# One Haar axis moved from TensorE to VectorE, whole 256-point transforms by channel, and plain products and sums for GpSimd in between

**Chip, cores, metric.** The kernel runs on one core of a Trainium2 chip, in fp32. The metric is the device time of one execution in microseconds (us); smaller is better. Every time is a median of several executions of one program. Runs have a state (fast or slow, by the clock that was granted).

## The reference

Four layers act on x[4, 64, 256, 256] one after the other. Layers 0, 2 and 3 are long convolutions of each image; layer 1 thresholds in the Haar domain.

```python
def _L0_conv_ref(x, ...):                      # layers 2 and 3 alike
    hx, hy = _implicit_filter(...), _implicit_filter(...)   # small sine networks
    k = einsum('ijk,imk->ijmk', hx, hy)[0]     # an outer product for every channel
    y = irfft2(rfft2(x, s=(512, 512)) * k_f)[..., :256, :256]
    return y + x * bias[:, None, None]

def _L1_conv_ref(x, v, conv_w, tau):
    f1 = haar2d(x)                             # 256-point Haar, both axes
    acc = 0
    for i in range(2):
        f3 = f1 * v[i]                         # v, tau: [256, 256]
        f4 = einsum('bchw,oc->bohw', f3, conv_w[i])        # 64 channels mixed
        acc = acc + sign(f4) * relu(abs(f4) - tau[i])
    return haar2d(acc, inverse=True) + x
```

One step of the Haar transform replaces a row by the sums and the differences of its even and odd elements, times 1/sqrt(2), and goes on with the sums: 128 pairs, 64, ... 1.

## The kernel before

As the filters are outer products, a convolution is two triangular matrix products, one per axis. Data are transposed by each product that has the image as the stationary operand. There are three phases with DRAM between them. **A**, by channel (four images): layer 0 (stages a1, a2) and two 128-point Haar products (a3, a4). **B**, by rows of coefficients, with (2 row groups x 64 channels) on the partitions: the "butterflies" that make a 256-point transform of two halves, then the products with v, the mixing of channels on TensorE, the thresholds, the sums. **C**, by channel: the inverse Haar products and layers 2 and 3.

```python
# Phase A: four stages on TensorE, eight PSUM buffers with one tag
hr = keep("ah")
for b, ps in enumerate(stage("a3")):
    haar_stationary(ps, x1[b], haarT)          # contracts rows, transposes
    nc.scalar.copy(hr[b], ps)
for b, ps in enumerate(stage("a4")):
    haar_moving(ps, hr[b], haarT)              # contracts rows, keeps the layout
    nc.vector.tensor_copy(fs[:, b], ps)
...
# Phase B, one step: 2 rows of either group, four units of 128 x 1024; PSUM bufs=4
butterfly(ft, r0, "fwd")
for b in range(B):
    f1 = ft[:, 2 * b : 2 * b + 2]...
    for i in range(2):
        nc.gpsimd.tensor_tensor(f3, f1, vts[:, i, :], ALU.mult)
        ... matmul f4 <- mix, f3
        nc.scalar.activation(m, f4, AF.Abs)
        nc.scalar.activation(f4, f4, AF.Sign)
        nc.vector.tensor_tensor(m, m, vts[:, 2 + i, :], ALU.subtract)      # two SBUF inputs
        nc.vector.scalar_tensor_tensor(m, m, 0.0, f4, ALU.max, ALU.mult)
    nc.vector.tensor_tensor(acc, ms[0], ms[1], ALU.add)
    nc.gpsimd.tensor_tensor(gt..., acc, f1, ALU.add)
butterfly(gt, r0, "inv")
```

Tiles are named by a tag, and a tag has `bufs` buffers that are used in turn. The order of the instructions of each engine, and the waits, are made when the program is built: an instruction of a later step can be placed ahead of one that stands earlier in the text.

Of the kernel before, what the change touches and what calls it, by code (L numbers as in the profile page):

```python
"""Four sequence-mixing layers on images x[b, c, 256, 256].

Layers 0, 2 and 3 convolve each image with a filter that is an outer product
hx x hy (zero padded to twice the length, so nothing wraps): out = Tx X Ty^T + bias X
with lower triangular Toeplitz matrices. Layer 1 works in the Haar domain: the
256-point transform is two 128-point transforms and a butterfly between their
scaling coefficients, and as it is orthogonal, "inverse(acc) + x" is
inverse(acc + forward(x)).

Phase A, by channel: layer 0 and the 128-point transforms of both axes.  # L10
Phase B, by rows of coefficients, channels on partitions: the butterflies, the
channel mixing, the soft thresholds, the inverse's butterflies.
Phase C, by channel: the 128-point inverse transforms, layers 2 and 3.
A product with the image as the stationary operand contracts its rows and leaves
it transposed, so two of them treat both axes.
"""
# [10 lines left out]
F32 = mybir.dt.float32  # L27
# [11 lines left out]
# A filter's period in DRAM, zeros after it, and how often it stands there.  # L39
PERIOD = N + P  # L40
REPEATS = 23
ROWS = 2
# [10 lines left out]
def conv_haar_kernel(ctx: ExitStack, tc: tile.TileContext, x, zT, w1, wbd, cols, decay, bias, haar, mixT, vt, out):  # L53
# [5 lines left out]
    haar_sb = const.tile([P, 2, P], F32, tag="haar", name="haar_sb")  # L59
    nc.sync.dma_start(haar_sb, haar)  # L60
    haarT = haar_sb[:, 0, :]
    haarN = haar_sb[:, 1, :]
# [9 lines left out]
    coef = dram.tile([B, C, N, N], F32, tag="coef", name="coef")  # L72
    mixed = dram.tile([B, C, N, N], F32, tag="mixed", name="mixed")
    filt = [dram.tile([P, REPEATS, PERIOD], F32, tag=f"filt{l}", name=f"filt{l}") for l in range(NL)]

    # The filters of all layers: x networks on partitions 0-63, y networks on 64-127.
    with tc.tile_pool(name="mlp", bufs=1) as mp, tc.tile_pool(name="mlp_ps", bufs=2, space=PSUM) as mps:
# [12 lines left out]
        for layer in range(3):  # L90
# [12 lines left out]
            # u less the nearest multiple of 2 pi, for the sine's range.  # L103
# [17 lines left out]
    def load_toeplitz(pool, l, c):  # L121
        """T[a, (x y), i] = h[i - a], with zeros for i < a: row a = 8 * a1 + a2 starts
        a1 periods less 8 and a2 periods less 1 behind the filter's first."""
        t = pool.tile([P, 2, N], F32, tag=f"toep{l}", name=f"toep{l}_{c}")
        for w in range(2):
            start = (w * C + c) * REPEATS * PERIOD
            src = bass.AP(filt[l].tensor, filt[l].offset + start, [[PERIOD - 8, 16], [PERIOD - 1, 8], [1, N]])
            nc.sync.dma_start(t[:, w, :], src)
        return t

    def toeplitz(ps, data, t, which):
        """ps[:, m, i] = sum over a of data[a, m] h[i - a]."""
        for m in range(2):
            cut = bass.ts(m, P)
            nc.tensor.matmul(ps[:, m, :], data[:, 0, cut], t[:, which, :], start=True, stop=False)  # L135
            nc.tensor.matmul(ps[:, m, HALF:], data[:, 1, cut], t[:, which, :HALF], start=False, stop=True)  # L136

    def haar_stationary(ps, data, mat):
        """Contracts data's rows and transposes it."""
        for m in range(2):  # L140
            for k in range(2):
                nc.tensor.matmul(
                    ps[:, m, bass.ts(k, P)], data[:, k, bass.ts(m, P)], mat, start=True, stop=True
                )

    def haar_moving(ps, data, mat):
        """Contracts data's rows and leaves its layout."""
        nc.tensor.matmul(ps, mat, data, start=True, stop=True)  # L148

    def images(ap, c):  # L150
        return [ap[b, c].rearrange("(k p) j -> p k j", p=P) for b in range(B)]

    # Phase A
    with (
        tc.tile_pool(name="a_in", bufs=3) as pin,
        tc.tile_pool(name="a_mid", bufs=6) as mid,
        tc.tile_pool(name="a_out", bufs=2) as pout,
        tc.tile_pool(name="a_ps", bufs=8, space=PSUM) as pps,
    ):
        for c in range(C):  # L160
            t0 = load_toeplitz(pin, 0, c)
            xs = pin.tile([P, B, 2, N], F32, tag="x", name=f"x_{c}")
            for b, src in enumerate(images(x, c)):
                nc.sync.dma_start(xs[:, b], src)
            fs = pout.tile([P, B, 2, N], F32, tag="f", name=f"f_{c}")

            def stage(name):
                return [pps.tile([P, 2, N], F32, tag="ps", name=f"{name}_ps{b}_{c}") for b in range(B)]

            def keep(name):  # L170
                return [mid.tile([P, 2, N], F32, tag=name, name=f"{name}{b}_{c}") for b in range(B)]

            cols_i = keep("ay")
            for b, ps in enumerate(stage("a1")):
                toeplitz(ps, xs[:, b], t0, 0)
                nc.scalar.copy(cols_i[b], ps)  # L176
            x1 = keep("ax")
            for b, ps in enumerate(stage("a2")):
                toeplitz(ps, cols_i[b], t0, 1)
                nc.vector.scalar_tensor_tensor(x1[b], xs[:, b], bias_sb[:, c : c + 1], ps, ALU.mult, ALU.add)  # L180
            hr = keep("ah")
            for b, ps in enumerate(stage("a3")):
                haar_stationary(ps, x1[b], haarT)
                nc.scalar.copy(hr[b], ps)
            for b, ps in enumerate(stage("a4")):
                haar_moving(ps, hr[b], haarT)
                nc.vector.tensor_copy(fs[:, b], ps)  # L187
            for b, dst in enumerate(images(coef, c)):
                nc.gpsimd.dma_start(dst, fs[:, b])  # L189

    # Phase B: a coefficient row is l = (h g r), h the transform's half; partitions are (g c).
    W = 2 * ROWS * N

    def rows_of(ap, g, r0):
        """[c, (b h), ROWS * N] of coefficient rows h * 128 + g * 64 + r0 ..."""
        start = g * (HALF // 2) + r0
        return [
            ap[b].rearrange("c (h l) k -> c h (l k)", h=2)[:, :, start * N : (start + ROWS) * N] for b in range(B)
        ]

    with (
        tc.tile_pool(name="b_in", bufs=2) as pin,
        tc.tile_pool(name="b_mid", bufs=2) as mid,
        tc.tile_pool(name="b_out", bufs=2) as pout,
        tc.tile_pool(name="b_ps", bufs=4, space=PSUM) as pps,
    ):

        def butterfly(t, r0, name):
            """Sums and differences of the halves' scaling coefficients, on both axes, in place."""
            pairs = t.rearrange("p n r (t q) -> p (n r) t q", t=2)[:, :, :, 0]  # L210
            sd = mid.tile([P, B * 2 * ROWS, 2], F32, tag="sd", name=f"{name}_{r0}")
            nc.vector.tensor_tensor(sd[:, :, 0], pairs[:, :, 0], pairs[:, :, 1], ALU.add)
            nc.vector.tensor_tensor(sd[:, :, 1], pairs[:, :, 0], pairs[:, :, 1], ALU.subtract)
            nc.vector.tensor_copy(pairs, sd)  # L214
            if r0 == 0:
                rows = t.rearrange("p (b h) r k -> p b h r k", h=2)[:C, :, :, 0, :]
                rsd = mid.tile([C, B, 2, N], F32, tag="rsd", name=f"{name}_r", bufs=1)
                nc.vector.tensor_tensor(rsd[:, :, 0, :], rows[:, :, 0, :], rows[:, :, 1, :], ALU.add)
                nc.vector.tensor_tensor(rsd[:, :, 1, :], rows[:, :, 0, :], rows[:, :, 1, :], ALU.subtract)
                nc.vector.tensor_copy(rows, rsd)  # L220

        for step in range(HALF // 2 // ROWS):
            r0 = step * ROWS
            ft = pin.tile([P, B * 2, ROWS, N], F32, tag="ft", name=f"ft_{step}")
            vts = pin.tile([P, 4, W], F32, tag="vt", name=f"vt_{step}")
            for g in range(2):
                part = slice(g * C, (g + 1) * C)
                nc.sync.dma_start(vts[part].rearrange("p q w -> p (q w)"), vt[step, g].partition_broadcast(C))
                for b, src in enumerate(rows_of(coef, g, r0)):
                    nc.sync.dma_start(ft[part, 2 * b : 2 * b + 2].rearrange("p h r k -> p h (r k)"), src)  # L230
# [163 lines left out]
```

## Time and profile before

| | before |
|---|---|
| median | 4529.9 us (4527.8 to 4534.3, four runs beside the changed kernel) |
| phase A, first to last TensorE stage | 1121.7 us, 17.5 per channel |
| phase B, first product to last sum | 1480.9 us, 11.57 per unit of 128x1024 (128 units) |
| phase C | 1792.4 us, 28.0 per channel |

The prediction below shows the slices, the windows and the timeline of one step. Names in all views: PE is TensorE, PEld its loading of stationary operands, DVE VectorE, ACT ScalarE, POOL GpSimd, SPq and ACTq the queues from which transfers (DMA) are issued. PSUM is the memory that the products write, SBUF the one that holds the other tiles. Here are two groups of instructions of B that it quotes only as numbers. Columns: line, engine, operation, output and inputs with shapes, count | busy us in total, mean ns of one | idle time of the engine before them and what ended it.

```profile
L238 POOL TENSOR_TENSOR f<-ft,vt 128x1024 f32<-128x1024 f32 x256 | 688.4, 2725 | 59.7 <-DVE ft L214 33.5 <-DMA vt<-in_vt 26.1
...
L245 DVE TENSOR_TENSOR m<-m,vt 128x1024 f32<-128x1024 f32 x256 | 585.2, 2296 | 317.6 <-ACT m L243 316.7
```

A product on GpSimd takes 2725 ns in the mean and VectorE's subtraction 2296 ns. Both means hold time in which one waits for the other: unblocked, the same shapes take 2.34 and 1.21 us in the prediction's timeline.

### The profile page before, as it was taken

The page shows a single profiled execution, that of the slowest core. Times are in us where ns is not written, and L with a number is a line of the kernel's source. Part 1 is how long each engine was busy: PE and PEld are TensorE (multiplying, and loading weights), DVE is VectorE, ACT ScalarE, POOL GpSimd, SP SyncE. Part 2 cuts the span into 40 slices and gives each one's busy share as a digit, 9 for nine tenths or more (in the row PEclk, how much of TensorE's full clock was granted, in tenths as well). Part 3 has the DMA queues.
Part 4 walks back from the last instruction along what each step waited for, and adds up shares of the span by engine and source line. Part 5 has one row for each costly group of instructions (what it writes and reads, how often), then busy time and mean ns, then how long its engine had stood idle before and what let it go on. Part 6 is the DMA issues. An engine that isn't in the chain of part 4 may idle for free.

```text
span 4528.7 us, 48425 instructions
## 1 busy us (share of the span) xinstructions
PE 3563.7 (79%) x18456; PEld 2761.6 (61%) x18456; DVE 2025.9 (45%) x2149; ACT 1235.8 (27%) x1796; POOL 1448.1 (32%) x901
## 2 busy tenths in 40 slices
PE   3999999999743434444443438999999999999999
PEld 2888888888511111111111117888888888888888
DVE  2333333333387776767676772333333333333333
ACT  0222222222233333333232332222222222222222
POOL 0111111111276767677777760111111111111111
PEclk7999999999867777777676769999999999999999
DMA  5444444444544545454545524222222222223321
GB/s 186 140 133 138 135 134 139 133 140 131 136 115 127 151 121 157 112 157 121 146 132 136 142 78 136 94 94 94 94 96 94 94 94 94 96 96 95 97 95 52
DMA packets 324605, 538.07 MB, mean 119 GB/s; under 512 B 32342, under 2 KB 221815, under 8 KB 320280
## 3 DMA queue, kind: packets, MB, share of 16 engines
q1 hardware_dynamic: 246552, 333.59, 25.6%
q0 software_dynamic: 40960, 134.25, 8.8%
q10 hardware_dynamic: 36864, 67.13, 4.9%
q8 instruction: 150, 2.46, 0.2%
q14 instruction: 79, 0.65, 0.0%
HBM read 319.94 MB, written 214.89 MB: 118 GB/s over the span
## 4 chain that ended last, share of the span: by engine, by line
issue 67%; POOL 11%; DVE 11%; DMA 5%; PE 3%; ACTq 2%; ACT 2%; SPq 1%; POOLq 0%; DVEq 0%
DVE m L245 5%; POOL coef L189 4%; POOL out L302 4%; DMA mixed<-gt 3%; DVE m L246 3%; DVE acc L249 2%; POOL gt L250 2%; ACTq L257 2%; ACT m L243 1%; POOL f L238 1%; DMA filt<-padded 1%; PE f L241 1%; ACT f L244 0%; PE a_ps L135 0%; DMA vt<-in_vt 0%
## 5 line engine op out<-in xcount | busy, mean ns | idle before, releaser
L241 PE MATMUL f<-f,mix_sb 128*128 128x512 f32 x1024 | 638.5, 780 | 857.3 <-POOL f L238 595.2
L241 PEld LDWEIGHTS f<-f,mix_sb 128*128 128x128 f32 x1024 | 243.3, 251 | 1251.7 <-POOL f L238 655.3
L245 DVE TENSOR_TENSOR m<-m,vt 128x1024 f32<-128x1024 f32 x256 | 585.2, 2296 | 317.6 <-ACT m L243 316.7
L238 POOL TENSOR_TENSOR f<-ft,vt 128x1024 f32<-128x1024 f32 x256 | 688.4, 2725 | 59.7 <-DVE ft L214 33.5
L302 POOL DMA_DIRECT2D out<-o x256 | 185.7, 726 | 1624.8 <-DVE o L297 1622.9
L243 ACT ACTIVATE m<-f 128x1024 f32<-128x1024 f32 x256 | 261.8, 1023 | 1017.9 <-DMA mixed<-gt 603.2
L189 POOL DMA_DIRECT2D coef<-f x256 | 185.8, 726 | 1020.1 <-DVE f L187 994.5
L250 POOL TENSOR_TENSOR gt<-acc,ft 128x1024 f32<-128x1024 f32 x128 | 387.7, 3029 | 371.3 <-DVE acc L249 371.3
L180 DVE SCALAR_TENSOR_TENSOR ax<-x,bias_sb,a_ps 128x512 f32<-128x512 f32 x256 | 191.3, 747 | 528.4 <-PE a_ps L136 476.9
L297 DVE SCALAR_TENSOR_TENSOR cy<-cz,bias_sb,c1c_ps 128x512 f32<-128x512 f32 x256 | 191.3, 747 | 482.8 <-PE c1c_ps L136 482.8
L297 DVE SCALAR_TENSOR_TENSOR o<-cy,bias_sb,c2c_ps 128x512 f32<-128x512 f32 x256 | 191.3, 747 | 479.4 <-PE c2c_ps L136 479.4
L135 PE MATMUL a_ps<-toep,x 128*128 128x256 f32 x1024 | 307.8, 383 | 43.4 <-DMA x<-in_x 43.4
L246 DVE SCALAR_TENSOR_TENSOR m<-m,f 128x1024 f32<-128x1024 f32 x256 | 302.7, 1211 | 8.5
L135 PE MATMUL c2r_ps<-toep,cy 128*128 128x256 f32 x1024 | 306.0, 381 | 0.0
L135 PE MATMUL c2c_ps<-toep,ch 128*128 128x256 f32 x1024 | 306.0, 381 | 0.0
L135 PE MATMUL c1c_ps<-toep,ch 128*128 128x256 f32 x1024 | 306.0, 381 | 0.0
L135 PE MATMUL a_ps<-toep,ay 128*128 128x256 f32 x1024 | 306.0, 381 | 0.0
L135 PE MATMUL c1r_ps<-toep,cz 128*128 128x256 f32 x1024 | 305.9, 380 | 0.0
L286 DVE COPY cz<-c_ps 128x512 f32<-128x512 f32 x256 | 177.2, 692 | 286.9 <-PE c_ps L148 286.9
L187 DVE COPY f<-a_ps 128x512 f32<-128x512 f32 x256 | 177.1, 692 | 267.9 <-PE a_ps L148 267.9
L292 ACT COPY ch<-c2r_ps 128x512 f32<-128x512 f32 x256 | 149.8, 585 | 520.9 <-PE c2r_ps L136 520.9
L176 ACT COPY ay<-a_ps 128x512 f32<-128x512 f32 x256 | 149.8, 585 | 450.8 <-PE a_ps L136 450.8
(63 smaller groups left out, 5873.1 us busy)
## 6 DMA issues: line engine op xcount, KB each, us to landing
x<-in_x SPq DMA_DIRECT2D x256, 256.0 KB, 3.9
coef<-f POOLq DMA_DIRECT2D x256, 256.0 KB, 2.8
vt<-in_vt SPq DMA_DIRECT2D x64, 1024.0 KB, 8.2
ft<-coef SPq DMA_DIRECT2D x256, 256.0 KB, 5.6
mixed<-gt ACTq DMA_DIRECT2D x256, 256.0 KB, 5.6
g<-mixed SPq DMA_DIRECT2D x256, 256.0 KB, 4.1
out<-o POOLq DMA_DIRECT2D x256, 256.0 KB, 2.8
toep<-filt SPq DMA_DIRECT2D x384, 128.0 KB, 2.7
```

The source lines that it names most:

```text
L135: nc.tensor.matmul(ps[:, m, :], data[:, 0, cut], t[:, which, :], start=True, stop=False)
L180: nc.vector.scalar_tensor_tensor(x1[b], xs[:, b], bias_sb[:, c : c + 1], ps, ALU.mult, ALU.add)
L189: nc.gpsimd.dma_start(dst, fs[:, b])
L238: nc.gpsimd.tensor_tensor(f3, f1, vts[:, i, :], ALU.mult)
L241: nc.tensor.matmul(f4[:, bass.ts(j, 512)], mix_sb[:, i, :], f3[:, bass.ts(j, 512)], start=True, stop=True)
L243: nc.scalar.activation(m, f4, AF.Abs)
L245: nc.vector.tensor_tensor(m, m, vts[:, 2 + i, :], ALU.subtract)
L246: nc.vector.scalar_tensor_tensor(m, m, 0.0, f4, ALU.max, ALU.mult)
L250: nc.gpsimd.tensor_tensor(gt[:, 2 * b : 2 * b + 2].rearrange("p h r k -> p (h r k)"), acc, f1, ALU.add)
L286: nc.vector.tensor_copy(cur[b], ps)
L297: nc.vector.scalar_tensor_tensor(nxt[b], cur[b], bias_sb[:, at : at + 1], ps, ALU.mult, ALU.add)
L302: nc.gpsimd.dma_start(dst, os[:, b])
```

## The change

The intent: TensorE bounds A and C, so take a Haar product off it. The transform of one axis becomes sums and differences on VectorE, which is mostly idle there; the other axis becomes one whole 256-point product. The inverse of that axis is still two 128-point products, with one butterfly left in B's first step; otherwise B needs no butterflies, and its operands are arranged so that VectorE and GpSimd do not block each other.

```diff
 # A
+        x1 = mid.tile([P, M * 2, N], ...)        # four images together
         ... a1, a2 as before, now from PSUM tag "ps", bufs=4 ...
+        fw = mid.tile([P, M * 2, N], F32, tag="fw", bufs=2)
+        forward_free(mid, x1, fw, ...)           # 16 VectorE instructions in series:
+            # nc.vector.tensor_tensor(at, split(even), split(odd), ALU.subtract)
+            # nc.vector.tensor_tensor(s, even, odd, ALU.add)     128, 64, ... 1 pairs
+        ... ps = pps.tile([P, 2, N], F32, tag="ps", name=f"a3ps...")   # the same tag
+        nc.tensor.matmul(ps[...], fw[...], haarH_sb[:, k, :], start=k == 0, stop=k == 1)
-            haar_stationary(ps, x1[b], haarT)
-            haar_moving(ps, hr[b], haarT)
 # B: one row of either group a step, two units; rows lead in DRAM
-    coef = dram.tile([B, C, N, N], F32, ...)
+    coef = [dram.tile([C, P, NB, 2, N], F32, ...)]
+        ft = pin.tile([P, ROWS, NB, W], F32, tag="ft", bufs=2)
-        butterfly(ft, r0, "fwd")
-                    nc.scalar.activation(m, f4, AF.Abs)
-                    nc.scalar.activation(f4, f4, AF.Sign)
-                    nc.vector.tensor_tensor(m, m, vts[:, 2 + i, :], ALU.subtract)
-                nc.vector.tensor_tensor(acc, ms[0], ms[1], ALU.add)
+                    f4 = pps.tile([P, 2, W], F32, tag="f4", bufs=2)       # was 4
+                    nc.scalar.activation(sg, f4, AF.Sign)
+                    nc.scalar.activation(f4, f4, AF.Abs)
+                    nc.vector.tensor_tensor(f4, f4, us[...], ALU.subtract)  # one input in PSUM
+                nc.gpsimd.tensor_tensor(acc, ms[0], ms[1], ALU.add)
 # C
+        inverse_free(mid, gs, ci, ...)           # 16 VectorE instructions, ahead of c1
-            haar_moving(ps, d[b], haarN)
```

## The prediction

> **What bounds the kernel now.** I read the page's busy table and 40 slices first, then the busy time by windows, then the timelines of one channel of A and one step of B, then the groups by form and the waits.
>
> The slices show three stretches. In A (slices 2 to 11) and C (from 25) TensorE is at 9; in B between them it is at 3 to 7, and VectorE and GpSimd share the load:
>
> ```profile
> PE   3999999999743434444443438999999999999999
> DVE  2333333333387776767676772333333333333333
> POOL 0111111111276767677777760111111111111111
> ```
>
> The windows give A, B and C. TensorE is busy for the whole of A (1119.00 of 1119.00) and C (1786.83 of 1790.00) with the clock granted fully; in B no engine reaches 75%:
>
> ```profile
> 85.00:1204.00 1119.00, 1119.00 (x6651) 944.80 (x6651) 366.80 (x510) 299.60 (x512) 183.20 (x253) 1.00 0.42 134
> 1218.00:2718.00 1500.00, 638.46 (x1024) 243.34 (x1024) 1077.52 (x838) 482.88 (x512) 1076.09 (x384) 0.71 0.49 132
> 2736.00:4526.00 1790.00, 1786.83 (x10725) 1559.68 (x10724) 559.87 (x768) 447.74 (x765) 185.74 (x256) 1.00 0.29 92
> ```
>
> Engines there, in order: PE, PEld, DVE, ACT, POOL. The chain of waits repeats every 17.49 us in A and every 27.97 us in C, which is the time of one channel. Count the columns that stream through TensorE for one channel. A convolution stage of one image is 2 x (256 + 128) = 768, so four images take 3072. A Haar product with the image stationary is 4 x 128 per image, 2048 for four; one with the image moving is 512 per image, also 2048. A has two convolution stages and both products: 10240 columns in 17.49 us, 1.708 ns each. C has four stages and both products: 16384 in 27.97 us, 1.707 ns each. The same rate in both says that the columns, and nothing else, set A and C.
>
> B is 32 steps of 46.1 us (128 units of 128x1024: a unit is two products, one sum over the two mixings, one sum with the input). One step in the timeline, GpSimd first, then VectorE:
>
> ```profile
> 1422.62 21.43 POOL L238 TENSOR_TENSOR f<-ft,vt 128x1024 f32<-128x1024 f32 x8 [1.06 <-DVE ft L214]
> 1445.31 3.26 POOL L250 TENSOR_TENSOR gt<-acc,ft 128x1024 f32<-128x1024 f32 x1 [1.26 <-DVE acc L249]
> 1453.14 3.25 POOL L250 TENSOR_TENSOR gt<-acc,ft 128x1024 f32<-128x1024 f32 x1 [4.56 <-DVE acc L249]
> 1460.95 3.26 POOL L250 TENSOR_TENSOR gt<-acc,ft 128x1024 f32<-128x1024 f32 x1 [4.56 <-DVE acc L249]
> 1465.37 2.34 POOL L250 TENSOR_TENSOR gt<-acc,ft 128x1024 f32<-128x1024 f32 x1 [1.16 <-DVE acc L249]
> ...
> 1452.98 4.49 DVE L245 TENSOR_TENSOR m<-m,vt 128x1024 f32<-128x1024 f32 x2
> 1457.40 2.34 DVE L246 SCALAR_TENSOR_TENSOR m<-m,f 128x1024 f32<-128x1024 f32 x2
> 1459.66 1.21 DVE L249 TENSOR_TENSOR acc<-m,m 128x1024 f32<-128x1024 f32 x1
> ```
>
> GpSimd does its eight products in a row, then waits for VectorE before each last sum. VectorE's unit takes 7.8 us of this (4.49 + 2.34 + 1.21, a little overlapped). Of the two subtractions, one takes 1.21 and the other some 3.3 us: it waits for GpSimd. The multiplication L246, which reads one operand from PSUM, takes 1.21 every time. At the step's start VectorE idles, since ScalarE is issuing eight stores (9.47 us) before its first Abs:
>
> ```profile
> 1422.36 9.47 ACTq L257 DMA_DIRECT2D mixed<-gt  x8
> 1431.88 1.02 ACT L243 ACTIVATE m<-f 128x1024 f32<-128x1024 f32 x1 [21.08 <-POOL f L238]
> 1432.93 2.32 DVE L245 TENSOR_TENSOR m<-m,vt 128x1024 f32<-128x1024 f32 x1 [10.53 <-ACT m L243]
> ```
>
> So B is not bound by one engine but by a relay of VectorE, GpSimd and ScalarE, cut at every step.
>
> **What the Trainium skill says.** (1) "SBUF — State Buffer", Who interferes with whom: a VectorE instruction with two SBUF inputs contends with a GpSimd instruction that reads SBUF, and whichever starts second blocks wholly; with at most one SBUF input (outside the two-port modes) there is no contention. The trace agrees: L245 (two SBUF inputs) averages 2296 ns, L246 (one from PSUM) 1211 ns; the GpSimd sum takes 3.26 beside VectorE and 2.34 alone. (2) "VectorE: DVE Perf Modes", the perf-mode tier table: fp32 tensor_tensor runs at one element per cycle of 0.96 GHz. Agrees: successive 1024-wide instructions start 1.13 us apart, 1.067 of elements and 0.065 of fixed time. (3) "SBUF — State Buffer", Door 1, says that four-byte elements lose nothing to a stride while two accesses fall on a 16-byte line; the new even/odd operands have stride 2. No run here shows it yet; the long strided operations aren't in this kernel. (4) "DMA: Bandwidth & Descriptors", Latency and other measured facts: DRAM rows whose pitch per partition is a large power of two are slower, 207 GB/s at 512 KiB and 164 at 2 MiB. B's new layout has a pitch of 1 MiB between channels. No run here shows this either.
>
> **The change part by part.**
>
> *A.* The second Haar product on TensorE goes, and the first becomes a full 256-point transform: 4 x 129 columns per image, 2064 for four. Columns: 6144 + 2064 = 8208, times 1.708 = 14.02 us per channel, 3.47 less; 64 channels: 897 us, 222 less. VectorE gets sixteen additions and subtractions over 8 rows: 2 x 8 x 255 = 4080 elements per partition, 4.25 us, and 16 x 0.065 to 0.1 us fixed, 5.6 us together. With four convolution evictions at 747 ns it has 8.6 us of work in 14.0, so it isn't the bound. But these sixteen stand in series between the last eviction and the transform, over all four images at once, so TensorE must have the next channel's first stage (3072 columns, 5.25 us) to do meanwhile. The buffers allow it (inputs 2, PSUM 4, next stage 5), and the order is made at build time by readiness: in B the eight products stand before the first sum, though the program alternates them. I take 0.4 us of unfilled wait per channel, 26 us, and 6 us for the last channel.
>
> *C.* The moving product goes: 12288 + 2048 = 14336 columns, 24.48 us, 3.49 less; 1567 us in all, 223 less. VectorE has 8 x 0.747 + 5.6 = 11.6 of 24.5 us. The inverse needs only the loaded coefficients, so it can run a channel ahead. I add 0.3 us per channel, 20 us.
>
> *B.* Same 128 units. The sum of the two mixings moves to GpSimd: four instructions of 2.34 us, about 2.30 start to start when none blocks (21.43 / 8 = 2.68 holds the blocked ones). VectorE's subtraction now reads PSUM, as the multiplication did, so none of its instructions has two SBUF inputs any more: 4 x 1.13 to 1.21 = 4.7 us per unit. ScalarE: 4 x 1.02 plus one store issue per unit at about 1.2 (9.47 / 8), 5.3 us. TensorE: eight passes at 0.43 to 0.85, at most 6.8 us. GpSimd at 4 x 2.30 = 9.2 is the bound: 128 units make 1178 us. To this I add 72 us for the wait of each sum on the one before it and for imperfect filling, 1250, against 1481 from first product (1233) to last sum (2714). The butterflies on VectorE at each step, which tie one step's start to the last one's end, are gone. [...]
>
> *Between.* Start to A as now, 86. A's end to the first product: 27 us now, of which much is vt loading, which can come during A; 18. Last sum to C: 22 now; fewer stores but an inverse of 5.6 us first; 20.
>
> Sum: 86 + (897 + 26 + 6) + 18 + 1250 + 20 + (1567 + 20) + 3 for the end = 3893. I predict 3900 us, 14% less.
>
> **The rivals.** *TensorE waits for VectorE.* If the order were the program's own, TensorE would stand for some 6 us per channel in A (64 x 5.6 = 360 us) and, with the inverse behind the last eviction of the channel before, again in C (as much): 3893 + 720 = 4610, slower than now. For it: the operands span all four images, each engine works in order. Against: B's order as above, and the buffers. Only A so: about 4230. *GpSimd is starved.* PSUM holds two mixing outputs instead of four. A mixing occupies its bank for 1.7 to 3.4 us of TensorE, 2.0 of ScalarE, 2.4 of VectorE and waits, 6.6 to 8.3, so two banks give one per 3.3 to 4.2 us, a unit per 6.6 to 8.3: just enough. If steps don't overlap, a step of two units lasts 9.4 us of products, some 8 of latency and the last sums, about 22 instead of 18.7: B 1410, total 4050. *Transfers.* B's 3 MB a step in 19 us is some 165 GB/s, against 132 now at a share of 0.49, and near what (4) gives for the pitch; if it bound, B would gain nothing beyond perhaps 100 us, total 4020. Against: pieces are larger and a third of it is a broadcast of few rows. *Nothing lost anywhere:* 86 + 903 + 15 + 1190 + 18 + 1567 + 3 = 3780.
>
> **Range and chances.** The low end is the sum without losses, 3780. The high end, 4110, holds a starved GpSimd or a partial wait in A, not both whole. Slower needs TensorE standing in both A and C: 0.04. Within 2% needs about half of that and a starved B: 0.04. Faster: 0.92.
>
> **What would show it right or wrong.** Right: a channel every 14.0 to 14.6 us in A and 24.5 to 25 in C, TensorE near its whole time in both; additions of the transform with mean times that sum to 5.6 us per channel; in B GpSimd above 90% with nearly every operation at 2.34, VectorE's subtraction at 1.2 instead of 2.3, and a unit per 9.3 to 9.9 us. Wrong: TensorE waiting for VectorE's transform with several us per channel; strided additions well over 1.2 us; GpSimd waiting for VectorE or loads; GpSimd operations above 2.4 us without a VectorE instruction of two SBUF inputs beside them.

## The result

The changed kernel took **4988.2 us** (4985.3 to 4990.1, four runs) against 4529.9 us: a ratio of 1.1007, with a 95% interval of 1.0992 to 1.1023. It is 10% slower; 3900 us had been predicted. Ratios here are taken over fast runs of the same batch; they are not quite the ratio of the medians quoted.

The phases, by the first and last instruction of each in the traces, beside the terms of the predicted sum:

| | predicted | changed | off by |
|---|---|---|---|
| start to A | 86 | 82.2 | -4 |
| A | 929 (14.5 per channel) | 1533.0 (23.95) | **+604** |
| A to B | 18 | 15.1 | -3 |
| B | 1250 (9.8 per unit) | 1763.2 (13.77) | **+513** |
| B to C | 20 | 17.7 | -2 |
| C | 1587 (24.8 per channel) | 1572.8 (24.57) | -14 |
| end | 3 | 4.3 | +1 |
| sum | 3893 | 4988.3 | +1095 |

So two terms are wrong, by 604 and 513 us, and C is right. The slices of the changed kernel (40 equal parts of the span; each digit is a busy share in tenths; PEclk is TensorE's granted clock in tenths):

```profile
PE   3677667776676454444444445457999999999999
...
POOL 0000000000000666666676766661000000000000
PEclk9888888888888666666666766668999999999999
```

In A (slices 2 to 13) TensorE was to stand at 9 and stands at 6 to 7, at a clock of 8. In B GpSimd was to stand at 9 and stands at 6 to 7. The windows of A, B and C (time and length, then busy us of PE, PEld, DVE, ACT, POOL with counts; granted clock; DMA share; GB/s):

```profile
85.00:1612.00 1527.00, 1065.59 (x6119) 1003.20 (x6119) 580.42 (x1280) 323.64 (x509) 0.00 (x0) 0.85 0.29 98
1700.00:3300.00 1600.00, 748.84 (x923) 257.30 (x922) 561.90 (x462) 443.17 (x462) 1069.08 (x462) 0.65 0.41 114
3420.00:4980.00 1560.00, 1560.00 (x10170) 1456.65 (x10169) 730.11 (x1488) 446.68 (x763) 0.00 (x0) 1.00 0.32 105
```

C is bound by TensorE alone, as before, with fewer columns. In A and in B no engine is near its whole time: there each phase waits for something once per channel or per step.

**One channel of A**, from the timeline (start, length, engine, line, operation; in brackets the idle time just before and what ended it):

```profile
502.31 0.39 PE L161 MATMUL a2ps<-toep,ay 128*128 128x128 f32 x2
...
503.52 1.23 DVE L179 TENSOR_TENSOR fw<-x 128x1024 f32<-128x1024 f32 x1
...
509.67 0.17 DVE L185 TENSOR_TENSOR fw<-f_17s 128x8 f32<-128x8 f32 x1
...
509.90 6.21 PE L247 MATMUL a3ps<-haarH_sb,fw 128*128 128x129 f32 x32 [7.21 <-DVE fw L185]
...
515.95 0.60 PE L160 MATMUL a1ps<-toep,x 128*128 128x256 f32 x2
```

TensorE ends a2 at 502.7 and does nothing for 7.21 us, until VectorE's last difference. VectorE itself needs 6.3 us (503.52 to 509.84) for its sixteen instructions, where 5.6 were estimated; the last eviction before them (0.75 us) and the hand-overs are the rest of the wait. The next channel's a1 comes after a3, at 515.95, though its inputs have long been loaded. And a3 takes 6.21 us where its 2064 columns at 1.708 ns would take 3.5. The granted clock, by windows of the same channel (columns as above, the clock third from the end):

```profile
502.31:509.90 7.59, 0.39 (x3) 0.22 (x2) 6.83 (x17) 0.00 (x0) 0.00 (x0) 0.88 0.55 173
509.90:512.00 2.10, 2.10 (x10) 2.10 (x11) 0.00 (x0) 0.00 (x0) 0.00 (x0) 0.50 0.00 0
512.00:514.00 2.00, 2.00 (x11) 2.00 (x11) 0.00 (x0) 0.97 (x2) 0.00 (x0) 0.50 0.00 0
514.00:516.10 2.10, 2.10 (x16) 2.10 (x16) 0.00 (x0) 1.09 (x2) 0.00 (x0) 0.79 0.00 0
516.20:526.00 9.80, 9.80 (x62) 9.05 (x61) 2.17 (x3) 2.97 (x5) 0.00 (x0) 1.00 0.26 107
```

After the pause the clock is 0.50 for 5.0 us: 4.1 in the two full windows, and 0.9 of the third, whose mean is 0.79 (taking the clock as 0.50 or 1.00 at any moment). Likewise the mean of 0.88 in the first window puts the fall at about 508.1, 5.4 us after TensorE's last product. The Trainium skill says in "TensorE: Matmul & The Clock Gate", Part 1: The HAM clock gate, that the clock halves after at least one idle window of about 3.4 us and is back after at least one busy one, and that the windows run freely, so that the delay varies. The 5.4 and 5.0 us here fit "at least one"; the 3.4 itself is not measured by any run. The prediction did not use it.

**One step of B**, from the timeline:

```profile
2302.81 6.95 POOL L282 TENSOR_TENSOR f<-ft,v 128x1024 f32<-128x1024 f32 x3 [9.20 <-DMA ft<-coef]
...
2319.16 2.34 POOL L296 TENSOR_TENSOR gt<-acc,ft 128x1024 f32<-128x1024 f32 x1
...
2321.53 1.08 SPq L273 DMA_DIRECT2D ft<-coef  x2
...
2330.09 6.96 POOL L282 TENSOR_TENSOR f<-ft,v 128x1024 f32<-128x1024 f32 x3 [8.59 <-DMA ft<-coef]
```

A step lasts 27.3 us, 18.7 of it work on GpSimd, as computed. At 2321.5 GpSimd ends the last sum that reads an input buffer ft, at 2321.53 the load into that buffer is issued, and the next instruction in GpSimd's order is the product that needs this load: 8.59 us later. There are two such buffers. But the built order runs a step ahead, products before the sums of the step before, so both are in use at that point. The operations themselves are as predicted (groups, columns as above):

```profile
L282 POOL TENSOR_TENSOR f<-ft,v 128x1024 f32<-128x1024 f32 x256 | 595.2, 2347 | 2180.3 <-DMA ft<-coef 2073.2
...
L289 DVE TENSOR_TENSOR f<-f,tau 128x1024 f32<-128x1024 f32 x256 | 314.9, 1230 | 1131.3 <-ACT f L288 1131.3
```

The product fell from 2725 to 2347 ns, the subtraction from 2296 to 1230. Of the 2073.2 us of waiting, 1629.3 are phase A, before the first product; the rest, 443.9, falls on 49 products. Waits before 13 others, 107.1 us and up to 9.0 each, are put down to TensorE, which reads the product's output buffer.

### The profile page after: what moved, and what is told of

The parts are those of the page before. It is cut to its first block, busy times and chain, and to the rows that moved or that the text cites. A ratio compares the mean times of both kernels' runs of the same rounds, so it can differ in the third digit from the quotient of the medians.

```text
span 4988.3 us, 46480 instructions
## 1 busy us (share of the span) xinstructions
PE 3488.8 (70%) x17432; PEld 2771.5 (56%) x17432; DVE 1975.9 (40%) x3363; ACT 1270.5 (25%) x1796; POOL 1187.0 (24%) x517
## 4 chain that ended last, share of the span: by engine, by line
PE 54%; POOL 21%; DVE 10%; DMA 10%; issue 4%; SPq 1%; ACT 0%; ACTq 0%; POOLq 0%; DVEq 0%
DMA ft<-coef 9%; POOL f L282 9%; PE a3ps L247 8%; POOL gt L296 6%; POOL acc L295 6%; PE c1ps L327 5%; PE a1ps L160 5%; PE c2c L160 4%; PE c1r L160 4%; PE c1c L160 4%; PE c2r L160 4%; PE a2ps L160 4%; DVE fw L179 4%; PE a2ps L161 2%; PE a1ps L161 2%
## 5 line engine op out<-in xcount | busy, mean ns | idle before, releaser
L282 POOL TENSOR_TENSOR f<-ft,v 128x1024 f32<-128x1024 f32 x256 | 595.2, 2347 | 2180.3 <-DMA ft<-coef 2073.2
L289 DVE TENSOR_TENSOR f<-f,tau 128x1024 f32<-128x1024 f32 x256 | 314.9, 1230 | 1131.3 <-ACT f L288 1131.3
L247 PE MATMUL a3ps<-haarH_sb,fw 128*128 128x129 f32 x2048 | 397.8, 383 | 461.4 <-DVE fw L185 461.4
L247 PEld LDWEIGHTS a3ps<-haarH_sb,fw 128*128 128x128 f32 x2048 | 387.4, 296 | 471.8 <-issue 471.8
L160 PE MATMUL a1ps<-toep,x 128*128 128x256 f32 x1024 | 308.5, 383 | 36.7 <-DMA toep<-filt 36.7
L292 DVE SCALAR_TENSOR_TENSOR m<-f,m 128x1024 f32<-128x1024 f32 x256 | 313.5, 1225 | 17.5
L160 PE MATMUL c1r<-toep,cz 128*128 128x256 f32 x1024 | 306.1, 381 | 0.0
L160 PE MATMUL c2c<-toep,ch 128*128 128x256 f32 x1024 | 306.1, 381 | 0.0
L160 PE MATMUL a2ps<-toep,ay 128*128 128x256 f32 x1024 | 306.1, 381 | 0.0
L160 PE MATMUL c1c<-toep,ch 128*128 128x256 f32 x1024 | 306.1, 381 | 0.0
```

Source lines behind the costliest of these rows:

```text
L160: nc.tensor.matmul(ps[:, m, :], data[:, 0, cut], t[:, which, :], start=True, stop=False)
L247: nc.tensor.matmul(ps[:, e, k * (HALF - 1) : k * (HALF - 1) + SPLIT], fw[:, 2 * (n + e) + k, bass.ts(m, P)], haarH_sb[:, k, :], start=k == ...
L282: nc.gpsimd.tensor_tensor(f3, f1, vs[:, r, i : i + 1, :].to_broadcast([P, 2, W]), ALU.mult)
L289: nc.vector.tensor_tensor(f4, f4, us[:, r, i : i + 1, :].to_broadcast([P, 2, W]), ALU.subtract)
L292: nc.vector.scalar_tensor_tensor(sg, f4, 0.0, sg, ALU.max, ALU.mult)
```

## The experiments

Twelve kernels were run, in four batches, each batch on one chip beside the kernel before. All gave right results. The numbers of theories in the expectations follow the order in which they were formed. Unless a line says otherwise, an experiment is an edit of the changed kernel, and "unit" is the time from B's first product to its last sum over 128.

### Is it the order in A?

Theory: buffers of one tag are handed out in the order of the text, so the next channel's a1, which follows a3 there, cannot be built ahead of it; a3 waits for VectorE, and a1 behind it. Rival: there are merely too few PSUM buffers. Another rival: the sixteen instructions are too slow and would bind whatever the order.

**a_split**: the same four buffers, but a3 has its own tag with two, and a1 and a2 share the other two.

```diff
-  a1ps, a2ps: tag="ps"  (bufs=4 of the pool)      a3ps: tag="ps"
+  a1ps, a2ps: tag="ps", bufs=2                    a3ps: tag="ps3", bufs=2
```

> Changed kernel, but in A the transform's PSUM tiles have a tag of their own (two buffers) and the convolutions' two, instead of four shared. Theory 1 (shared PSUM buffers are handed out in program order, so the next channel's first stage can't stand before this channel's transform on TensorE, which waits 7.2 us for VectorE and then runs its transform at a lowered clock): the built order now has the next first stage and part of the second before the transform, so a channel of A falls from 23.9 us to 14.1-15.0, the transform from 6.2 to about 3.5 us, the granted clock in A returns to 1.0; total 4988 - 64 x 9.3 = about 4390. Rival 1a (the 129-column transform with its overlapping PSUM columns is slow by itself, not the clock): the wait goes but the transform stays at 6.2 us, a channel is 16.7 us, total about 4530. Rival 1b (strided VectorE work is what limits A): little change, above 4800.

Measured: 4412.1 us, ratio 0.9735 (0.9715 to 0.9754); A has 14.78 us per channel instead of 23.95, B is nearly unchanged (13.89 us per unit, 13.77 before). The timeline of TensorE in the same stretch:

```profile
503.86 0.60 PE L160 MATMUL a1ps<-toep,x 128*128 128x256 f32 x2
...
511.13 3.99 PE L247 MATMUL a3ps<-haarH_sb,fw 128*128 128x129 f32 x32
514.96 0.39 PE L161 MATMUL a2ps<-toep,ay 128*128 128x128 f32 x2
```

The next channel's a1, and part of its a2, now stand ahead of a3, which waits for nothing and runs at a granted clock of 1.00 (in 3.99 us, not the 3.5 of its columns; the half microsecond is not explained). VectorE does the same sixteen instructions as before; they are hidden.

**a_ps8**: one tag as in the changed kernel, but eight buffers (B's PSUM is taken only after A's is given back).

```diff
-  b_pools = pools(bs, "b", 2);  a_pools = pools(s, "a", 4)
+  a_pools = pools(s, "a", 8);  ...A...;  s.close();  b_pools = pools(bs, "b", 2)
```

> Changed kernel, but A has eight PSUM buffers under the one shared tag (B's pool is opened only after A), as the kernel before had. Theory 1, sharpened (buffers of one tag are handed out in the program's order at first use, so the order is fixed by the shared tag and not by how many buffers there are): the built order of TensorE is unchanged, a channel of A stays at 23.9 us, TensorE's wait at 7.2 us, total 4960-5020. Rival 1c (four buffers are too few, eight would let the next stage run ahead): a channel falls to about 14.5 us and the total to about 4400.

One run of 5017.3 us, state unknown; A has 23.90 us per channel, and the wait in the list of waits (total us, times, longest) is the changed kernel's to the tenth:

```profile
PE a3ps L247 <- DVE fw L185: 461.4, 64, 7.2
```

So four more buffers of the same tag do nothing, and two tags with no buffer more do everything. That tags are handed out in the order of the text is my reading of these two runs; that the number of buffers is not the cause is shown.

**a_warm**: the order left as it is, but TensorE does seven idle products in the wait (fourteen in the trace, as each fp32 product is recorded twice), whose results nobody reads.

```diff
-  a1ps, a2ps, a3ps: tag="ps"  (bufs=4 of the pool)
+  a1ps, a2ps, a3ps: tag="ps", bufs=3           # to make room for "warm"
+  wm = pps.tile([P, 2, N], F32, tag="warm", bufs=1)
+  for n in range(7):
+      nc.tensor.matmul(wm, ay[3][:, 0, 0:P], ay[n % M], start=True, stop=True)
```

> Changed kernel, but seven unused 512-column products per channel of A (6.1 us) stand on TensorE in the time in which it waits for VectorE's transform. They make nothing and shorten no wait; they only keep TensorE busy. Theory 5 (of the 9.9 us that a channel of A lost against the prediction, 2.7 us are the lowered clock after the idle 7.2 us: granted 0.50 for some 4 us): the transform on TensorE falls from 6.2 to 3.5-3.7 us, a channel from 23.9 to 21.2-21.4, the total by 160-175 us to about 4820. Rival (the transform is slow for another reason, its overlapping PSUM columns or cold data): it stays at 6.2 us and the total at 4980 or more.

Measured: 4844.9 us, 1.0694 (1.0678 to 1.0710) of the kernel before; A has 21.53 us per channel, a little more than the 21.2 to 21.4 expected. From its timeline:

```profile
502.18 2.74 PE L241 MATMUL warm<-ay,ay 128*128 128x512 f32 x6
...
509.54 3.81 PE L250 MATMUL a3ps<-haarH_sb,fw 128*128 128x129 f32 x32 [1.19 <-DVE fw L185]
```

With TensorE busy through the wait, a3 takes 3.81 us, not 6.21. That is 2.4 us less, close to the 2.5 that 5.0 us at half the clock would lose (an estimate from the windows above); that the shared tag has three buffers here does not change the order in the timeline. The excess of a channel of A is thus made of 7.2 us of waiting and 2.4 us of halved clock: 14.0 + 7.2 + 2.4 = 23.6, measured 23.95; the last 0.3 is left open.

### Is it the load in B?

Theory: the ft buffer. Rivals: the power-of-two pitch of 1 MiB between channels in DRAM, which slows the load; the two PSUM buffers; the sum on GpSimd.

**b_ft3**: one more input buffer.

```diff
-  ft = pin.tile([P, ROWS, NB, W], F32, tag="ft", bufs=2)
+  ft = pin.tile([P, ROWS, NB, W], F32, tag="ft", bufs=3)
```

> Changed kernel, but three buffers instead of two for B's coefficient loads. Theory 2 (GpSimd's product for the next step stands right behind the sum that frees the buffer its input is loaded into, so each step waits for a whole load, 8.6 us, with GpSimd in order): the load is asked for one step earlier and hidden; a step falls from 27.3-27.7 us to 18.7-20, B from about 1770 to 1200-1290, total about 4480. Rival 2 (transfers can't come faster, by rate or by row pitch): the wait only moves, a step stays at 24 us or more, total above 4750.

Measured: 4465.0 us, 0.9851 (0.9836 to 0.9865); the unit fell from 13.77 to 9.70 us. In its list of waits, the one for the load is left only at the start of B:

```profile
POOL f L282 <- DMA ft<-coef: 1624.7, 1, 1624.7
```

**b_pad**: the pitch between channels in DRAM made 1 MiB + 8 KiB, ft left at two buffers.

```diff
-  coef = [dram.tile([C, P, NB, 2, N], ...)]            # and mixed
+  coef = [dram.tile([C, P + 1, NB, 2, N], ...)[:, :P]]  # and mixed
```

> Changed kernel, but 8 KB of padding between the channels of both coefficient arrays in DRAM (pitch 1 MiB + 8 KiB). Theory 2 (the wait is the latency of one load asked for too late, not a rate): landing of the coefficient loads at 5.2 us as now or within 1 us of it, a step of B at 26.5-27.7 us, total 4940-4990. Rival 2 (the power-of-two pitch slows the transfers): landing falls by 2 us or more, a step by as much, total below 4860.

Measured: 4993.6 us, 1.1018 (1.1001 to 1.1034), the unit 13.81, and the loads land after 5.2 us in the median in both kernels: nothing changed. The pitch is not the cause; the fourth place from the skill in the prediction had no weight here.

**ab**: a_split and b_ft3 together, to see whether the two account for the whole.

> Both edits, a_split and b_ft3. If both theories hold the parts add: 4988 - 600 - 510 = about 3880, which is the prediction on record (3900); A 14.1-15.0 us a channel, B 18.7-20 us a step, C 24.5-25 us a channel as now. If the rivals hold, above 4300.

Measured: 3879.8 us (3878.4 to 3880.7), 0.8559 (0.8546 to 0.8572). A 14.78 per channel, B 9.70 per unit, C 24.56. The two corrections split one PSUM tag in two and raise one number from two to three, and they turn 10% slower into 14% faster.

### What is each part of B's arithmetic worth?

**bef_barith**: the kernel before, with only the new arithmetic of B (subtraction in PSUM, sum on GpSimd).

```diff
-  nc.scalar.activation(m, f4, AF.Abs);   nc.scalar.activation(f4, f4, AF.Sign)
-  nc.vector.tensor_tensor(m, m, vts[:, 2 + i, :], ALU.subtract)
-  nc.vector.scalar_tensor_tensor(m, m, 0.0, f4, ALU.max, ALU.mult)
+  nc.scalar.activation(m, f4, AF.Sign);  nc.scalar.activation(f4, f4, AF.Abs)
+  nc.vector.tensor_tensor(f4, f4, vts[:, 2 + i, :], ALU.subtract)
+  nc.vector.scalar_tensor_tensor(m, f4, 0.0, m, ALU.max, ALU.mult)
...
-  nc.vector.tensor_tensor(acc, ms[0], ms[1], ALU.add)
+  nc.gpsimd.tensor_tensor(acc, ms[0], ms[1], ALU.add)
```

> Kernel BEFORE with only B's arithmetic of the change: Sign to SBUF, Abs and the subtraction in PSUM, the sum of the two mixings on GpSimd; layout, transforms and steps as before. Theory 3 (VectorE's subtraction was blocked by GpSimd because both its inputs were in SBUF): the subtraction falls from 2296 to about 1230 ns, GpSimd's products from 2725 to 2345 and its sums from 3029 to 2345; GpSimd then has 16 x 2.3 = 37 us in a step of B, and a step falls from 46.1 to 38-41 us, total 4290-4400. Rival 3 (the sixteen products and sums of GpSimd and the stores' issue set the step anyway, so that moving a sum to GpSimd costs what the contention gave): a step at 44-47 us, total 4480-4560.

Measured: 4311.5 us, 0.951 (0.9496 to 0.9524); the unit 9.83 instead of 11.57. Its groups:

```profile
L238 POOL TENSOR_TENSOR f<-ft,vt 128x1024 f32<-128x1024 f32 x256 | 594.1, 2357 | 56.4 <-DVE ft L214 30.5 <-DMA vt<-in_vt 25.9
...
L245 DVE TENSOR_TENSOR f<-f,vt 128x1024 f32<-128x1024 f32 x256 | 314.6, 1229 | 465.5 <-ACT f L244 440.2 <-PE f L241 12.6 <-DMA mixed<-gt 6.9
```

Beside the same two lines of the kernel before, 368 ns of a product and 1067 ns of a subtraction are gone; layout, transforms and steps are as before, and the sum of the mixings has moved to GpSimd. That is the reading of "SBUF — State Buffer", Who interferes with whom, in the prediction: a VectorE instruction with one SBUF input does not contend with GpSimd.

**bef_bsub**: the same without the last two lines, so the sum of the two mixings stays on VectorE.

> Kernel BEFORE with Sign to SBUF, Abs and the subtraction in PSUM, but the sum of the two mixings left on VectorE. Theory 3: the subtraction is free of blocking (1230 ns instead of 2296); the sum on VectorE still has two SBUF inputs and blocks and is blocked (1.2 to 3.4 us); GpSimd has twelve instructions a step (27.6 us plus blocking), VectorE 4 x (4.7 + 1.2 to 3.4). With GpSimd relieved of four sums a step should be no longer than with them, 35-40 us against 39.3 in bef_barith, total 4150-4340. Rival: the blocking of the sum costs what it saves, a step at 40-44 us, total 4340-4470.

Measured: 4280.6 us, 0.9444 (0.9428 to 0.9460); the unit 9.61. A product takes 2362 ns and the subtraction 1224, as in bef_barith, so the subtraction alone carries the gain; the sum on GpSimd adds nothing and costs a little. It makes GpSimd the bound: 4 x 2.35 = 9.4 us a unit.

### Can it be made better?

**overlap**: ab with the images in two groups, so that one group's B runs beside the other's A and C.

```diff
-GROUPS = 1
+GROUPS = 2
+  # after each channel pair of A (or C) of one group, the steps of B of the other
```

> ab with two groups of images (a parameter the kernel has) and B of the first group written between the channels of A of the second, B of the second between the channels of C of the first. TensorE sets A and C, GpSimd sets B, so beside each other they should cost the longer of the two: A of group 0 460 us, A of group 1 beside B of group 0 650-800 (GpSimd 64 x 9.6 = 614), C of group 0 beside B of group 1 900-1000 (TensorE 784 + 112), C of group 1 784, total 3000-3300. Rival 5 (VectorE's transforms have two SBUF inputs, so they and GpSimd block each other, and TensorE waits): total 3400-3800.

Measured: 3857.6 us, 0.8517 (0.8491 to 0.8543): hardly better than ab, far from the hoped-for 3000 to 3300 and even above the 3400 to 3800 of the rival. VectorE's transforms have two SBUF inputs, and GpSimd now works beside them (timeline of VectorE, with one line of GpSimd):

```profile
786.07 2.71 DVE L179 TENSOR_TENSOR fw<-f_12s 128x512 f32<-128x512 f32 x1
...
838.33 2.34 POOL L296 TENSOR_TENSOR gt<-acc,ft 128x1024 f32<-128x1024 f32 x1
838.41 2.30 DVE L184 TENSOR_TENSOR fw<-f_14s 128x8 f32<-128x8 f32 x1
```

In the changed kernel, where GpSimd rests in A, these VectorE shapes take 0.69 and 0.17 us. The 128x8 difference starts 0.08 us after a GpSimd sum of 2.34 us and ends with it: a short instruction can wait for a whole GpSimd instruction. VectorE's busy time rises from 1967 us in ab to 2461. The kernel also moves 657 MB instead of 539, as filters, v and tau are loaded once for each group. How much of the missed gain is the blocking and how much the loads, for which GpSimd waits again, is not settled.

**ab_accdve**: ab with the sum of the two mixings back on VectorE, to relieve GpSimd: 3 x 2.34 = 7.0 us a unit.

```diff
-  nc.gpsimd.tensor_tensor(acc, ms[0], ms[1], ALU.add)
+  nc.vector.tensor_tensor(acc, ms[0], ms[1], ALU.add)
```

> ab with one part undone: the sum of the two mixings back on VectorE. Theory 4 (in ab GpSimd's four instructions of 2.3 us are the bound of B and VectorE has room): GpSimd has three, 6.9 us, and some blocking comes back since the sum has two SBUF inputs; a unit of B falls from 9.6 to 7.5-8.8 us, B by 100-260 us, total 3620-3780. Rival 4 (blocking eats it, the choice of GpSimd for the sum was right): a unit at 9.3 us or more, total above 3830.

Measured: 3812.2 us (3809.9 to 3813.5), 0.8408 (0.8394 to 0.8422), the unit 9.17: better, and a miss, as less than expected. Its groups:

```profile
L282 POOL TENSOR_TENSOR f<-ft,v 128x1024 f32<-128x1024 f32 x256 | 618.4, 2432 | 1110.2 <-DMA ft<-coef 1041.6 <-PE f L285 51.2 <-issue 17.3
...
L295 DVE TENSOR_TENSOR acc<-m,m 128x1024 f32<-128x1024 f32 x128 | 183.0, 1430 | 8.7
```

Some of the contention is back (2432 ns against 2348 in ab). The larger part is idle time: GpSimd is busy for 912 us in the whole program, and B lasts 1174 us.

**ab_accdve_f4**: ab_accdve with four PSUM buffers for the mixings instead of two (theory: a mixing holds its buffer too long for two).

```diff
-  f4 = pps.tile([P, 2, W], F32, tag="f4", bufs=2)
+  f4 = pps.tile([P, 2, W], F32, tag="f4", bufs=4)      # B's PSUM taken after A's
```

> ab_accdve, but each phase's pools are opened when the one before has closed, so that B has four PSUM buffers for the mixings' outputs instead of two (C keeps four of one bank). Theory 6 (with the sum on VectorE, B at 9.17 us a unit is bound by the two PSUM buffers: one mixing holds its buffer through TensorE, two ScalarE and two VectorE passes, and TensorE waits 456 us for VectorE to free one): a unit falls to 7.3-8.2 us, B by 120-240 us; some 10-30 us come back at the phase ends, where nothing can be loaded ahead; total 3600-3720. Rival (blocking between the sum and GpSimd is the bound): a unit stays above 8.8 us, total above 3780.

Measured: 3880.1 us, 0.8562 (0.8549 to 0.8575), the unit 9.62: worse, so the theory fell as it stood. (The edit also opens the pools of each phase only after the phase before; the start and the gaps between phases grow by 7 us in all, of the 68 lost.) The timeline shows why:

```profile
1500.48 1.08 SPq L273 DMA_DIRECT2D ft<-coef  x2
...
1509.31 6.96 POOL L282 TENSOR_TENSOR f<-ft,v 128x1024 f32<-128x1024 f32 x3 [4.24 <-issue]
```

With more PSUM buffers the built order runs one more step ahead, and three ft buffers are again one too few: the load is issued at 1500.48, right after the sum that frees its buffer (ended at 1500.4), and the product that needs it starts at 1509.31, after 4.24 us of nothing. The profile puts this wait down to "issue"; that it is the load was an inference until the next run.

**ab_accdve_f4ft4**: the same with four ft buffers.

```diff
-  ft = pin.tile([P, ROWS, NB, W], F32, tag="ft", bufs=3)
+  ft = pin.tile([P, ROWS, NB, W], F32, tag="ft", bufs=4)
```

> ab_accdve_f4 with the input buffers of B's coefficients four deep instead of three. Theory 7 (the fourth PSUM buffer let the built order run one step further ahead, and it then met the coefficient buffer, which was freed right before it was asked for: GpSimd idles 4.2 us a step, and each step waits a load): with one buffer more than the run-ahead the wait goes, a unit of 128 falls from 9.62 us to 7.3-8.0, and the total to 3600-3700 us. Rival (VectorE's sums and GpSimd's products hold each other up at the SBUF, or the next load, v or tau, takes the place): the unit stays at 8.8 us or above and the total above 3780 us.

Measured: **3667.3 us** (3666.2 to 3668.9), 0.8093 (0.8079 to 0.8106), the unit 7.98, at the upper end of what was expected. GpSimd's timeline has no gap any more:

```profile
1500.53 3.34 POOL L296 TENSOR_TENSOR gt<-acc,ft 128x1024 f32<-128x1024 f32 x1
1503.84 2.35 POOL L282 TENSOR_TENSOR f<-ft,v 128x1024 f32<-128x1024 f32 x1
...
1508.45 7.94 POOL L282 TENSOR_TENSOR f<-ft,v 128x1024 f32<-128x1024 f32 x3
...
1499.62 2.04 DVE L295 TENSOR_TENSOR acc<-m,m 128x1024 f32<-128x1024 f32 x1
...
1507.24 2.34 DVE L295 TENSOR_TENSOR acc<-m,m 128x1024 f32<-128x1024 f32 x1
```

So the fourth PSUM buffer was right and useless alone. What remains is contention: the first sum takes 3.34 us and three products 7.94 instead of 2.34 and 6.95, each time beside VectorE's sum of two SBUF inputs (the last two lines). GpSimd's mean times of 2608 ns (256 products) and 2797 ns (128 sums) make 1026 us, and B lasts 1022: it is bound by GpSimd, with some 125 us of blocking in it (1026 less 384 x 2.345). This version beats both kernels: it takes 19% less time than the kernel before and 26% less than the change as made (3667.3 over 4988.2, medians of different batches).

## Why the prediction was wrong

**A: the step "The buffers allow it (inputs 2, PSUM 4, next stage 5), and the order is made at build time by readiness" failed.** The dependence had been seen: the sixteen instructions stand in series before a3, and TensorE must have other work. That it would have it was concluded from the number of buffers and from B, where products are built ahead of sums. But B's products and sums write tiles of different tags; in A the three stages share one, and a_split and a_ps8 show that this decides the order. The rival "TensorE waits for VectorE" had named the case: some 6 us per channel, "Only A so: about 4230", with too small a chance: "slower" was tied to A and C together, and it came of A and B. It was also sized too small: b_ft3, which has the wait in A alone, took 4465. The wait was put at 5.6 us and is 7.2; the clock that it costs, 2.4 us, was in no term. Together 9.6 us in 64 channels are 614 us, where the term is off by 604.

**B: the durations were right, the order's second effect was left out.** GpSimd's 2.34 us, VectorE's 1.2, contention gone, a unit of 9.3 to 9.9: all came true once the load was out of the way (9.70). The step that failed is "To this I add 72 us for the wait of each sum on the one before it and for imperfect filling": the 4.07 us per unit that b_ft3 takes away are 521 us, a wait that the list had no term for. "Transfers" was a rival as a rate, and the rate did not bind (114 GB/s in B, no effect of the pitch, and 195 GB/s in B of ab_accdve_f4ft4 with the same layout). What bound is when a load may begin. The same build order that was counted on to fill the engines consumes buffers: a product that runs one step ahead needs an input buffer more. "GpSimd is starved" (160 us at most in B, where 513 were lost) had the right engine and the wrong buffer, PSUM; with ft at three, two PSUM buffers carried 9.70.

**C: right.** 24.57 us per channel against 24.48 by columns and 24.8 with the allowance. There nothing of the same channel precedes the VectorE series but a load, so the inverse is computed a channel ahead.

**Strides: right.** The even and odd operands have stride 2, and their 1024-wide additions take 1.22 and 1.23 us, as unit stride does. "SBUF — State Buffer", Door 1, says so for four-byte elements, and the trace agrees.

With A and B corrected the whole sum holds: ab took 3879.8 us, against 3893 worked out (A 946 us against 929, B 1241 against 1250, C 1572 against 1587: small errors of either sign). The mechanism of the gain had been read correctly, and the conditions under which it is had were not.

## What to carry to other kernels

When a change puts a serial chain on another engine between two stages of TensorE, look which instructions can be built ahead of the waiting stage, tag by tag; give the waiting stage its own buffers, and count a long wait of TensorE twice, as time and as clock (7.2 us cost 2.4 more here). An input buffer must be free a whole load before it is asked for: here it took one buffer more than the steps that the order keeps open at once (three with two steps open, four with three, as I read the timelines), and a deeper PSUM made that number larger. The repeated gap in a phase where no engine is full told more here than any engine's mean. The skill names the sign ("Perfetto Trace Analysis", Optimization Strategy: the same gap repeating can mean that the next tile has no room); b_ft3 agrees, a_ps8 shows that more room is not always what is lacking.

## What the Trainium skill lacked or had wrong

- No page tells that stages sharing one tag keep each other's order: 23.90 us per channel with eight shared buffers, 14.78 with four in two tags. "Perfetto Trace Analysis", Optimization Strategy, has the symptom and names too little room as a possible cause, which was not the cause in A.
- No page ties the depth of input buffers to how far the order runs ahead: 13.77 us per unit with two ft buffers and 9.70 with three; with four PSUM buffers 9.62 with three and 7.98 with four.
- "SBUF — State Buffer", Who interferes with whom, agrees with the runs, but has no example of what a short instruction pays: a 128x8 difference took 2.30 us instead of 0.17 beside GpSimd.
- "DMA: Bandwidth & Descriptors", Latency and other measured facts, has 207 GB/s at a pitch of 512 KiB and 164 at 2 MiB, and nothing on 1 MiB; here padding that pitch by 8 KiB changed nothing (13.77 and 13.81 us per unit) while 114 GB/s were moved. Unpadded, B of ab_accdve_f4ft4 moved 195 GB/s; no run padded the pitch at such a rate.
- "TensorE: Matmul & The Clock Gate", Part 1, had what the prediction lacked: 7.2 us of idle time gave a clock of 0.50 for 5.0 us of the work that followed. Its examples are a wait for DMA and cycling through PSUM; none is a wait for VectorE, which did the same here.
